# Edge counts in a graph network: own buffers, and a new spread of 565 small steps over three stages of the second layer's experts

## The chip, the cores and the metric

The kernel runs on one core of a Trainium2 chip. The metric is the device time of one execution in microseconds; lower is better. A core has five engines that run their own instruction streams in order: TensorE (PE, matrix products), VectorE (DVE), ScalarE (ACT), GpSimd (POOL) and SyncE (SP, which issues most transfers).

## The reference, cut to what matters

Four layers work on 3125 nodes with 256 features; each has a graph part over 50000 edges and a feed-forward part. The change touches the feed-forward part of the second layer and the counts that the graph part of the third layer needs.

```python
# second layer, feed-forward: the two best of 8 experts for each node
gate_logits = xf @ Wg + bg
top_w, top_i = jax.lax.top_k(gate_logits, 2)
top_w = softmax(top_w)
for e in range(8):
    h = gelu(xf @ W1[e] + b1[e])             # 256 -> 1024
    out += w_dense[:, e] * (h @ W2[e] + b2[e])   # 1024 -> 256

# third layer, graph: four convolutions over the same edges and self loops
deg = zeros(n).at[dst].add(1.0);  norm = rsqrt(deg)[src] * rsqrt(deg)[dst]
segment_sum((h @ W)[src] * norm[:, None], dst)
```

The third layer does not gather the edges again. It uses a table `c.adj` that holds, for each pair of source node and target node, how many edges join them (plus 1 on the diagonal for the self loop), and multiplies by it.

## The kernel before, in words

Nodes are kept in 25 tiles of 128 rows (`NT`, `P`), the running features in `c.x`.

*Feed-forward part of layer two* (`l1_ffn`). A row normalisation (`layernorm`) leaves `ys` and its transpose `c.yT`. `logits_of` computes the gate, `top8` picks the experts, and `route` works out, mostly on DVE, at which row of a buffer in DRAM each node's copy for its first and second expert belongs. `scatter_rows` then writes the rows there: 50 indirect transfers (`tbuf<-ys`), issued one after the other by POOL. `moe` walks over 32 blocks of 256 rows (`NS`, `ST`). Per block SP loads the expert's weights (`wa`, `wb`, 1 MB each) and the rows (`bx`); PE transposes the rows (`pbx`), DVE copies them to SBUF (`bT`); PE makes eight hidden chunks (`ph`, in `hidden`), ACT applies the gelu (`hT`); PE makes two output tiles of 8 products each (`po`), DVE adds the bias (`yo`), SP stores it (`obuf`). In the trace every such product of float32 data shows as two matmul records. After the loop 50 indirect fetches (`vr<-obuf`), issued by POOL, bring each node's two results back, and DVE adds them to `c.x`. After that the third layer begins with the row statistics of `c.x` (lines 158 and 159).

*Edge counts* (`adjacency`). 565 slots (`NSLOT`) of 128 edge records each have to be counted. A slot is a small chain: ACT makes `cdiff` and `cfrom` (one-hot rows of the sources), DVE makes `cto` (one-hot rows of the targets), PE multiplies them (`pcnt`, one record, 512 columns). The first 175 slots (`NFIX`) go to fixed places of `c.adj`: ACT writes the table. The other 390 go to places read from a list: DVE loads six registers at a time (`groups_of`) and adds the slot to the table with a read and a write (line 961). `work` is a Python generator: each `next(side, None)` emits one slot at that place of the program.

What sets the order: the text of the program gives the order of emission, and a scheduler of the framework then orders each engine's instructions by its own estimates, so that a slot can stand some way before or after the place where it was emitted. Before the change `moe` emits slots only in the block loop: one after each hidden chunk, one after every second product of an output tile and one after each tile, 18 per block, so that they run out in the last block. The slots' buffers (`cdiff` 3, `cfrom` and `cto` 6 each, `pcnt` 2 in PSUM) lie in the pools `wp` and `pp` of `moe`, in memory that `ys` held until the scatters had read it.

Of the kernel before, what the change touches and what calls it, by code (L numbers as in the profile page):

```python
# [17 lines left out]
PSUM = bass.MemoryType.PSUM  # L18
# [39 lines left out]
NFIX = NT * NDS  # L58
NMORE = (E - 1) // P
NSLOT = NFIX + NMORE  # L60
LOG2 = math.log(2.0)
BIG = 1.0e30
GROUP_BOUND = "a node tile's index is a sum of at most 24 comparisons"
# [695 lines left out]
def moe(c, I, pre, rows, exi, w0, w1, hid, beside=None):  # L759

    nc, tc = c.nc, c.tc
    w1n, b1n, w2n, b2n = pre
    mc = hid // P
    SR = ST // P
    with tc.tile_pool(name="moe1", bufs=1) as cp:
        with tc.tile_pool(name="moeps0", bufs=1, space=PSUM) as pp:
            b1 = load_cols(c, cp, pp, I[b1n], "b1c")
        with tc.tile_pool(name="moe", bufs=2) as wp, tc.tile_pool(name="moeps", bufs=2, space=PSUM) as pp:  # L770
            side = beside(wp, pp) if beside else iter(())
            for b in range(NS):
                (es,) = groups_of(c, exi, b, 1, SPE, NEXP - 1)
                (ev,) = groups_of(c, exi, b, 1, DVE, NEXP - 1)
                wa = wp.tile([P, KD, hid], F32, name="ew1")
                wb = wp.tile([P, mc, D], F32, name="ew2")
                b2 = wp.tile([P, D], F32, name="eb2")
                nc.sync.dma_start(
                    wa, I[w1n][bass.ds(es, 1)].rearrange("o (c p) n -> p (o c) n", p=P)
                )  # L780
                nc.sync.dma_start(
                    wb, I[w2n][bass.ds(es, 1)].rearrange("o (c p) n -> p (o c) n", p=P)
                )
                nc.sync.dma_start(b2, I[b2n][bass.ds(es, 1)].to_broadcast([P, D]))
                bc = wp.tile([P, mc], F32, name="eb1")
                nc.vector.tensor_copy(bc, at(b1.rearrange("p (e m) -> p e m", m=mc), ev))
                bT = wp.tile([P, KD, ST], F32, name="bT")
                for s in range(SR):
                    bx = wp.tile([P, D], F32, name="bx", bufs=4)
                    r0 = b * ST + s * P  # L790
                    nc.sync.dma_start(bx, c.tbuf[r0 : r0 + P, :])
                    pt = pp.tile([P, KD, P], F32, name="pbx", bufs=2)
                    for k in range(KD):
                        nc.tensor.transpose(pt[:, k, :], bx[:, k * P : (k + 1) * P], c.ident)
                    nc.vector.tensor_copy(bT[:, :, s * P : (s + 1) * P], pt)  # L795
                hT = wp.tile([P, mc, ST], F32, name="hT")
                for m in range(mc):
                    hidden(
                        c, pp, hT, wa, bT, ST, m,
                        lambda o, i, m=m, bc=bc: nc.scalar.activation(o, i, AF.Gelu, bias=bc[:, m : m + 1]),  # L800
                        bufs=2,
                    )
                    next(side, None)
                for s in range(SR):
                    po = pp.tile([P, D], F32, name="po", bufs=2)
                    for m in range(mc):
                        nc.tensor.matmul(po, hT[:, m, s * P : (s + 1) * P], wb[:, m, :], start=(m == 0), stop=(m == mc - 1))  # L807
                        if m % 2:
                            next(side, None)
                    next(side, None)  # L810
                    yo = wp.tile([P, D], F32, name="yo", bufs=4)
                    nc.vector.tensor_add(yo, po, b2)
                    r0 = b * ST + s * P
                    nc.sync.dma_start(c.obuf[r0 : r0 + P, :], yo)
            for _ in side:
                pass
        with tc.tile_pool(name="moer", bufs=8) as wp:
            for t in range(NT):
                for ri, w in zip(rows, (w0, w1)):
                    v = wp.tile([P, D], F32, name="vr")  # L820
                    gather(c, v, c.obuf, ri[:, t : t + 1])
                    xt = c.x[:, t, :]
                    nc.vector.scalar_tensor_tensor(xt, v, w[:, t : t + 1], xt, op0=OP.mult, op1=OP.add)
# [88 lines left out]
def adjacency(c, keep):  # L912

    nc, tc = c.nc, c.tc
    W = DS * P
    c.adj = keep.tile([P, NT * NT + DS - 1, P], U8, name="adj")
    nc.gpsimd.memset(c.adj[:, NT * NT :, :], 0.0)
    rec = keep.tile([P, NSLOT, 4], F32, name="crec_s")
    nc.sync.dma_start(rec, c.rec_c[: NSLOT * P, :].rearrange("(p k) w -> p k w", p=P))
    ui = keep.tile([1, NSLOT], I32, name="cui")  # L920
    nc.vector.tensor_copy(ui, rec[0:1, :, 2])
    io = keep.tile([P, W], BF16, name="ciota")
    nc.gpsimd.iota(io, pattern=[[1, W]], base=-W // 2, channel_multiplier=0, allow_small_or_imprecise_dtypes=True)
    is_ = keep.tile([P, P], BF16, name="ciotas")
    nc.gpsimd.iota(is_, pattern=[[1, P]], base=0, channel_multiplier=0, allow_small_or_imprecise_dtypes=True)

    def work(wp, pp):
        def counts(k, n):

            d = wp.tile([P, P], BF16, name="cdiff", bufs=3)  # L930
            nc.scalar.activation(d, is_, AF.Abs, bias=rec[:, k, 0:1])
            a = wp.tile([P, P], BF16, name="cfrom", bufs=6)
            nc.scalar.activation(a, d, AF.Relu, bias=1.0, scale=-1.0)
            b = wp.tile([P, W], BF16, name="cto", bufs=6)
            nc.vector.tensor_scalar(b[:, :n], io[:, :n], rec[:, k, 1:2], None, op0=OP.is_equal)
            ps = pp.tile([P, W], F32, name="pcnt", bufs=2)
            return ps, a, b

        for g in range(NT):
            for s in range(NDS):  # L940
                nd = min(DS, NT - s * DS)
                n = nd * P
                ps, a, b = counts(g * NDS + s, n)
                own = g // DS == s
                nc.tensor.matmul(ps[:, :n], a, b[:, :n], start=True, stop=not own)
                if own:
                    o = (g % DS) * P
                    nc.tensor.matmul(ps[:, o : o + P], c.identb, c.identb, start=False, stop=True)
                d0 = g * NT + s * DS
                nc.scalar.activation(  # L950
                    c.adj[:, d0 : d0 + nd, :].rearrange("p a d -> p (a d)"), ps[:, :n], AF.Identity
                )
                yield
        for k0 in range(NFIX, NSLOT, 6):
            regs = groups_of(c, ui, k0, 6, DVE, NT * NT - 1)
            for j in range(6):
                ps, a, b = counts(k0 + j, W)
                nc.tensor.matmul(ps, a, b, start=True, stop=True)  # L958
                o = c.adj[:, bass.ds(regs[j], DS), :].rearrange("p a d -> p (a d)")

                nc.vector.scalar_tensor_tensor(o, o, 100.0, ps, op0=OP.min, op1=OP.add)  # L961
                yield

    return work
# [452 lines left out]

def l1_ffn(c, I, keep):
    nc, tc = c.nc, c.tc
    beside = adjacency(c, keep)  # L1420
    with tc.tile_pool(name="f1", bufs=1) as cp:
        w0 = cp.tile([P, NT], F32, name="w0")
        w1 = cp.tile([P, NT], F32, name="w1")
        with tc.tile_pool(name="f1y", bufs=1) as yp:
            ys = yp.tile([P, NT, D], F32, name="ys")
            c.yT = yp.tile([P, KD, NP], F32, name="yT")
            layernorm(c, residual=False, ys=ys)
            wg = load_w(c, yp, I["L1_ffn_Wg"], "wg")
            bg = load_rows(c, yp, I["L1_ffn_bg"], "bg")
            lg = logits_of(c, yp, wg, bg, "lg1f")  # L1430
            mx, xf = top8(c, yp, lg)

            ex = yp.tile([P, NT], F32, name="ex2")
            nc.vector.tensor_sub(ex, mx[:, :, 1], mx[:, :, 0])
            nc.scalar.activation(ex, ex, AF.Exp)
            nc.vector.tensor_scalar_add(w0, ex, 1.0)
            nc.vector.reciprocal(w0, w0)
            nc.vector.tensor_mul(w1, ex, w0)
            rows, to, exi = route(c, cp, xf)
            scatter_rows(c, ys, to, "L1 tokens")  # L1440
        moe(c, I, ("L1_ffn_W1", "L1_ffn_b1", "L1_ffn_W2", "L1_ffn_b2"), rows, exi, w0, w1, 1024, beside)


def aggregate(c, wp, pp, acc, table, f):
# [606 lines left out]
```

## Time and profile before

| | us |
|---|---|
| median of 3 runs | 6873.1 (6866.4 to 6880.27) |
| profiled execution, its own time | 6859.87 |
| span of the profiled execution | 6858.1 |
| first scatter of layer two issued | at 3833.15 |
| last scatter issued | at 3895.15 |
| first hidden product of the experts | at 3912.99 |
| last `yo` of the experts begins | at 4535.1 |
| last of the 50 fetched results is added, begins | at 4603.45 |

The last five rows are times from the start of the span, read from the timeline. Between the first scatter and the last added result lie 770 us, a ninth of the span. Busy times and waits of an engine are read within that stretch; the whole page's shares average over four layers with different limits.

### The profile page before, as it was taken

To read this page: it belongs to the slowest core of one execution; us is meant where nothing else is said; L and a number is where in the kernel's file an instruction comes from. 1 tells how busy PE (TensorE), PEld (TensorE's weight loads), DVE (VectorE), ACT (ScalarE), POOL (GpSimd) and SP (SyncE) were. 2 spreads that over 40 slices of the span, in tenths; PEclk is the share of its full clock that TensorE was granted. 3 is DMA by queue.
4 is the path that set the end of the run, shared out by engine and by line. 5 is a ranking of instruction groups with operands and counts; after the bars stand their busy time and mean duration, and the time that the engine had idled before them with its cause. 6 is when DMAs were issued, how large, how long until landed. Compare 5 with 4: busy or idle time off the path is not lost. (4 is left out here: it accounts for less than half of the span.)

```text
span 6858.1 us, 79775 instructions
## 1 busy us (share of the span) xinstructions
PE 5098.2 (74%) x22936; PEld 3293.1 (48%) x22945; DVE 3956.1 (58%) x11222; ACT 2190.3 (32%) x6415; POOL 2873.3 (42%) x2832
## 2 busy tenths in 40 slices
PE   5778877885225688888885499947989996777594
PEld 3334333463114455555552377734755554444353
DVE  7555665463613578888886248867421114787503
ACT  3223333201001355555552297731212232000120
POOL 2566666677452177777762200020000002777101
PEclk8667787798568888888885699978988998788697
DMA  8323444371226322222221244430000001445232
GB/s 211 96 93 123 149 146 127 129 246 62 98 77 192 107 68 70 68 70 68 70 48 39 96 144 139 141 102 1 1 2 18 10 10 57 129 130 124 74 98 62
DMA packets 386625, 634.00 MB, mean 92 GB/s; under 512 B 72756, under 2 KB 273816, under 8 KB 378886
## 3 DMA queue, kind: packets, MB, share of 16 engines
q1 hardware_dynamic: 248386, 348.59, 16.4%
q0 software_dynamic: 118368, 259.84, 14.2%
q10 hardware_dynamic: 19428, 20.37, 0.9%
q8 instruction: 191, 3.13, 0.2%
q14 instruction: 252, 2.06, 0.1%
HBM read 478.42 MB, written 150.13 MB: 92 GB/s over the span
## 5 line engine op out<-in xcount | busy, mean ns | idle before, releaser
L217 POOL DMA_INDIRECT g<-tab,src x880 | 893.1, 1015 | 474.7 <-issue 315.7
L566 PE MATMUL p<-wf,sT 128*128 128x256 f32 x1564 | 599.6, 511 | 175.8 <-DVE sT L198 103.6
L566 PEld LDWEIGHTS p<-wf,sT 128*128 128x128 f32 x1564 | 335.8, 242 | 422.8 <-DVE sT L198 155.1
L217 POOL DMA_INDIRECT g<-tab,idx x391 | 402.1, 1028 | 303.7 <-ACT brec L391 110.1
L335 POOL DMA_INDIRECT rec_c<-crec,cpos x440 | 450.7, 1024 | 134.1 <-issue 124.4
L335 POOL DMA_INDIRECT rec_a<-g,posi x391 | 403.0, 1031 | 220.6 <-issue 66.2
L1728 POOL MEMSET acc<- 128x6425 f32 x1 | 5.5, 5453 | 1122.4 <-DVE x L664 1122.4
L335 POOL DMA_INDIRECT rec_b<-brec,bpos x391 | 415.0, 1061 | 119.2 <-issue 119.2
L651 PE MATMUL ph<-bT,ew 128*128 128x256 f32 (+1 forms) x1536 | 436.4, 420 | 18.0 <-DVE bT L795 12.8
L217 POOL DMA_INDIRECT vr<-obuf,rri x100 | 95.1, 951 | 834.2 <-issue 826.9
L1096 DVE TENSOR_REDUCE tm<-pb 128x2 f32<-128x512 f32 x550 | 359.7, 682 | 33.6 <-PE pb L1092 33.5
L1595 PE MATMUL pagg<-t,adj 128*128 128x384 bf16 (+1 forms) x2500 | 341.4, 289 | 31.7 <-DVE t L1589 28.5
L651 PEld LDWEIGHTS ph<-bT,ew 128*128 128x128 f32 x1536 | 286.3, 191 | 149.8 <-issue 56.3
L664 DVE SCALAR_TENSOR_TENSOR x<-po,pr,x 128x256 f32<-128x256 f32 x200 | 94.3, 484 | 454.7 <-PE po L662 454.7
L1782 PE MATMUL ps<-g,oh 128*128 128x257 f32 x880 | 324.0, 523 | 20.2 <-DVE mrun L1103 11.4
L568 DVE SCALAR_TENSOR_TENSOR g<-p,wgt,g 128x256 f32<-128x256 f32 x391 | 187.0, 481 | 257.2 <-PE p L567 239.2
L807 PE MATMUL po<-ew,hT 128*128 128x256 f32 x1280 | 321.9, 380 | 0.0
L1296 ACT ACTIVATE g<-g 128x64 f32<-128x64 f32 x1320 | 320.8, 335 | 0.9
L1306 PE MATMUL ps<-g,oh 128*128 128x277 f32 x880 | 303.2, 481 | 15.0 <-ACT g L1296 7.0
L1280 PE MATMUL z<-xr,ohT 128*128 x1320 | 251.5, 298 | 69.5 <-DVE lrest L1010 50.5
L509 PE MATMUL p<-rT,wf 64*128 64x512 f32 x392 | 280.6, 822 | 28.3 <-DVE ssp_r L197 26.9
L961 DVE SCALAR_TENSOR_TENSOR adj<-adj,pcnt 128x512 f32 x390 | 266.6, 684 | 50.7 <-PE pcnt L958 40.9
(641 smaller groups left out, 11597.6 us busy)
## 6 DMA issues: line engine op xcount, KB each, us to landing
ew<-in_L_ffn_W_dram SPq DMA_DIRECT2D x64, 1024.0 KB
rb<-rec_a SPq DMA_DIRECT2D x55, 1032.0 KB
tt<-to_rows SPq DMA_DIRECT2D x110, 256.0 KB
a<-in_edge_attr_dram SPq DMA_DIRECT2D x85, 256.0 KB
ew<-in_L_ffn_w_dram SPq DMA_DIRECT2D x64, 256.0 KB
bx<-tbuf SPq DMA_DIRECT2D x128, 128.0 KB
obuf<-yo SPq DMA_DIRECT2D x128, 128.0 KB
ew<-in_L_ffn_w_dram SPq DMA_DIRECT2D x16, 1024.0 KB
```

What stands on the lines that cost most here:

```text
L217: return c.nc.gpsimd.indirect_dma_start(out=out, out_offset=None, in_=table, in_offset=bass.IndirectOffsetOnAxis(ap=idx, axis=0))
L335: st = nc.gpsimd.indirect_dma_start(out=rec, out_offset=bass.IndirectOffsetOnAxis(ap=posi[:, j : j + 1], axis=0), in_=rc[:, j, :], in_offs ...
L509: nc.tensor.matmul(p1, wf1[64 * h : 64 * h + 64, k * P : (k + 1) * P], rT[64 * h : 64 * h + 64, :], start=True, stop=True)
L566: nc.tensor.matmul(p2, sT[:, k, :], wf2[:, k, :], start=(k == 0), stop=False)
L651: nc.tensor.matmul(ph[:, :n], w[:, k, m * P : (m + 1) * P], inT[:, k, :], start=(k == 0), stop=(k == kc - 1))
L807: nc.tensor.matmul(po, hT[:, m, s * P : (s + 1) * P], wb[:, m, :], start=(m == 0), stop=(m == mc - 1))
L961: nc.vector.scalar_tensor_tensor(o, o, 100.0, ps, op0=OP.min, op1=OP.add)
L1096: nc.vector.tensor_reduce(to, pb.rearrange("p i k e -> p i (k e)"), AX.X, OP.max)
L1296: nc.scalar.activation(v[:, h, :], v[:, h, :], AF.Copy, scale=k.gh[:, j, h, C : C + 1])
L1306: nc.tensor.matmul(ps, oh[:, 2 * q + i, :], k.g[:, 2 * q + i, :], start=(i == 0), stop=(i == 1))
L1595: nc.tensor.matmul(ps, adj[:, g * NT + d, :], tab[:, g], start=(g == 0), stop=(g == NT - 1))
L1782: nc.tensor.matmul(ps, oh, k.g[:, j, :SW], start=(i == 0), stop=(i == 1))
```

## The change

The slots get pools of their own (`cw` in SBUF, `cps` in PSUM), opened in `l1_ffn` around everything, and the generator is handed to `moe` instead of being started there. 80 slots are emitted directly after the scatters (`SLOTS_FIRST`), 12 per block in the expert loop (384 together: one after each hidden chunk, and one after every fourth product of an output tile), and four before each tile's fetched results are added (100). What is left, one slot, follows at the end.

```diff
+SLOTS_FIRST = 80
 def moe(c, I, pre, rows, exi, w0, w1, hid, beside=None):
...
-            side = beside(wp, pp) if beside else iter(())
+            side = beside or iter(())
...
                         nc.tensor.matmul(po, hT[:, m, s * P : (s + 1) * P], wb[:, m, :], start=(m == 0), stop=(m == mc - 1))
-                        if m % 2:
+                        if m % 4 == 3:
                             next(side, None)
-                    next(side, None)
                     yo = wp.tile([P, D], F32, name="yo", bufs=4)
                     nc.vector.tensor_add(yo, po, b2)
                     r0 = b * ST + s * P
                     nc.sync.dma_start(c.obuf[r0 : r0 + P, :], yo)
-            for _ in side:
-                pass
         with tc.tile_pool(name="moer", bufs=8) as wp:
             for t in range(NT):
+                for _ in range(4):
+                    next(side, None)
                 for ri, w in zip(rows, (w0, w1)):
                     v = wp.tile([P, D], F32, name="vr")
                     gather(c, v, c.obuf, ri[:, t : t + 1])
...
 def l1_ffn(c, I, keep):
     nc, tc = c.nc, c.tc
-    beside = adjacency(c, keep)
+    with tc.tile_pool(name="cw", bufs=1) as wp, tc.tile_pool(name="cps", bufs=1, space=PSUM) as pp:
+        l1_ffn_beside(c, I, adjacency(c, keep)(wp, pp))
+
+
+def l1_ffn_beside(c, I, side):
...
             scatter_rows(c, ys, to, "L1 tokens")
-        moe(c, I, ("L1_ffn_W1", "L1_ffn_b1", "L1_ffn_W2", "L1_ffn_b2"), rows, exi, w0, w1, 1024, beside)
+            for _ in range(SLOTS_FIRST):
+                next(side, None)
+        moe(c, I, ("L1_ffn_W1", "L1_ffn_b1", "L1_ffn_W2", "L1_ffn_b2"), rows, exi, w0, w1, 1024, side)
+        for _ in side:
+            pass
```

The first layer's experts use the same `moe` without slots.

More of the change, by code (lines that the diff above doesn't have):

```diff
@@ L1419, in l1_ffn @@
     nc, tc = c.nc, c.tc
-    beside = adjacency(c, keep)
+    with tc.tile_pool(name="cw", bufs=1) as wp, tc.tile_pool(name="cps", bufs=1, space=PSUM) as pp:
+        l1_ffn_beside(c, I, adjacency(c, keep)(wp, pp))
+def l1_ffn_beside(c, I, side):
+    nc, tc = c.nc, c.tc
     with tc.tile_pool(name="f1", bufs=1) as cp:
```

## Prediction

> **What bounds the kernel now.** The page's chain of waits starts at 5094.94, after the stages that change, so I read them from the table by stretches, then the waits inside the expert loop, then the timeline for the time from one start to the next (the pitch), which is shorter than a duration where instructions overlap.
>
> ```profile
> 3833.00:3897.00 64.00, 0.00 (x0) 0.00 (x0) 0.86 (x6) 0.00 (x0) 48.03 (x50) 0.50 0.29 102
> 3897.00:3920.00 23.00, 13.01 (x41) 7.24 (x43) 7.46 (x25) 18.40 (x55) 0.00 (x0) 0.60 0.67 232
> 3920.00:4102.00 182.00, 178.46 (x840) 134.06 (x846) 67.22 (x211) 177.16 (x552) 0.00 (x0) 1.00 0.45 146
> 4102.00:4527.00 425.00, 405.22 (x1846) 306.88 (x1845) 374.53 (x878) 327.29 (x956) 0.00 (x0) 1.00 0.41 133
> 4540.00:4604.00 64.00, 0.00 (x0) 0.00 (x0) 29.85 (x83) 0.00 (x0) 46.31 (x49) 0.50 0.49 144
> ```
>
> Columns: length, then busy us of PE, weight loads, DVE, ACT, POOL, then PE's granted clock. Beside the scatters (row 1) only POOL works; in the expert loop (rows 3, 4) PE is full at clock 1.00; beside the fetches (row 5) POOL sets the pace, DVE is half free, PE and ACT are idle at clock 0.50. So the slots sit where PE has no room, and two stretches of 64 us stand nearly empty.
>
> ```profile
> DVE adj L961 <- PE pcnt L958: 40.5, 67, 0.9
> PE pcnt L958 <- DVE adj L961: 19.7, 65, 1.4
> PEld ph L651 <- DVE bT L795: 15.3, 20, 1.2
> ```
>
> Waits within row 4. 390 listed slots in groups of six make 65 register loads, and PE waits for DVE 65 times.
>
> ```profile
> 4303.53 0.68 DVE L961 SCALAR_TENSOR_TENSOR adj<-adj,pcnt 128x512 f32 x1
> 4304.13 0.35 DVE L935 TENSOR_SCALAR cto<-ciota,crec_s 128x512 bf16<-128x512 bf16 x1
> 4304.39 0.68 DVE L961 SCALAR_TENSOR_TENSOR adj<-adj,pcnt 128x512 f32 x1
> ...
> 4307.66 0.38 PE L958 MATMUL pcnt<-cto,cfrom 128*128 128x512 bf16 x1
> 4308.74 0.38 PE L958 MATMUL pcnt<-cto,cfrom 128*128 128x512 bf16 x1
> ...
> 4318.31 0.35 DVE L935 TENSOR_SCALAR cto<-ciota,crec_s 128x512 bf16<-128x512 bf16 x1
> 4319.56 0.69 DVE L961 SCALAR_TENSOR_TENSOR adj<-adj,pcnt 128x512 f32 x1 [0.90 <-PE pcnt L958]
> ...
> 4591.29 0.88 DVE L823 SCALAR_TENSOR_TENSOR x<-vr,w,x 128x256 f32<-128x256 f32 x2 [1.99 <-DMA vr<-obuf,rri]
> ```
>
> PE: four product records and one slot in 1.08 us, so 0.216 per record. DVE: `adj` 0.60 and `cto` 0.265 to the next start, 0.86 a slot; a result's addition 0.40 (0.88 for two of 0.48). Behind a register load `adj` comes 0.98 us later than DVE is free.
>
> ```profile
> 3961.83 0.54 ACT L933 ACTIVATE cfrom<-cdiff 128x128 bf16<-128x128 bf16 x2
> 3962.23 0.62 ACT L950 ACTIVATE adj<-pcnt 128x512 uint8<-128x512 f32 x1
> 3962.71 0.72 ACT L931 ACTIVATE cdiff<-ciotas,crec_s 128x128 bf16<-128x128 bf16 x2
> 3963.30 0.62 ACT L950 ACTIVATE adj<-pcnt 128x512 uint8<-128x512 f32 x1
> ```
>
> ACT per fixed slot: 0.20 + 0.48 + 0.295 = 0.975 us, about 0.95 with one narrow slot in seven.
>
> ```profile
> 3895.15 0.96 POOL L749 DMA_INDIRECT tbuf<-ys,rti  x1 [0.30 <-issue]
> 3911.23 1.11 PE L794 MATMUL pbx<-ident,bx 128*128 128x128 f32 x4 [2.85 <-DMA bx<-tbuf]
> 3912.99 3.02 PE L651 MATMUL ph<-bT,ew 128*128 128x256 f32 x8
> ```
>
> The experts start 17 us after the last scatter ends (3896.1): rows and weights have to land first.
>
> **The change, step by step.** The built program shows each engine's order. PE: 13 slots before the routing's products, 55 before the expert biases' transpose (`pcols`), 80 before the third hidden chunk, 463 before the last output product, 102 behind it. No matmul and no transfer is added; POOL's order is as before, SP only issues some row loads (`bx`) earlier.
>
> *Routing and scatters: +9.* The slots no longer wait for the scatters, so they mix into the normalisation and the routing. The first two `cdiff` pairs and `cfrom` stand before the normalisation's root on ACT, 7 `cto` (1.9 us) before its reciprocal on DVE: +2.4; ACT's copies of the transposed rows get 4 `adj`, 2 `cfrom`, 2 `cdiff` more: +3 in all. Before the routing's product PE has 9 more slots at ACT's pace (9 x 0.95 = 8.5, against 8 us that DVE needs there): +4.3 in all. 25 `cto` stand before the first scatter's index is ready, 28 before the second's. With 6 buffers, `cto` number k waits for product k-6, so DVE's routing, and with it POOL's queue, runs at ACT's slot pace: the second scatter starts 8.5 later.
>
> Here a rule speaks against the change: the Trainium skill, "SBUF — State Buffer", section "Who interferes with whom", has `tensor_scalar` in a two-port mode hold the port that GpSimd needs, one side blocking fully. No row shows `cto` beside POOL. The nearest is the first layer's scatters (1786 to 1860): with DVE 71.91 of 74 us busy on other forms, POOL issued 54 transfers, one per 1.37 us against 1.265 here. With about 30 `cto` (10 us busy) in 62 us the row gives 0.015 per scatter, +0.7; the rule at its worst 30 x 0.35 = +10. Below nothing it can't be. I take the row: +9; ends +3 and +20.
>
> *Expert stage: -39.* First the opening. `pcols` comes at 3909 and the rows at 3920 (the transfers are the same, 9 later); only 62 slots may stand ahead of the rows in PE's order, and before the third hidden chunk PE has 18 more slots at 0.95 plus ACT's table load and two gelus (2 us): 3939, 34 us after the last scatter, where 17 sufficed. From there PE has 2040 product records and 381 slots at 0.216 (523) and 116 transposes at an estimated 0.13 (15): 538. The same sum before, from 3912.99: 2048 and 553 records (562), 124 transposes (16), 1 for the diagonal: 579, against 622 measured, so 43 were stalls, 1.4 per block. With 12 slots instead of 18, and 1.9 us between slots in the output tiles, the waits behind register loads (19.7) nearly go; the wait for `bT` (about 0.5 per block: one bias addition 0.34, one `adj` 0.60, one copy 0.42 less the PE work in between) stays, and in the first eight blocks ACT needs 1.19 per hidden chunk against PE's 1.08. I take 0.9 per block, 28. Sum 34 + 566 = 600 against 639.4 from the last scatter to the last `yo`: -39; ends -84 (no stall, and the opening as before) and -22 (stalls as before).
>
> *Fetches and statistics: +56.* DVE's order from the last `yo` to the last row statistic holds 102 `adj` (61), 97 `cto` (26), 50 additions (20), 25 statistics (0.40 each, 10, all behind the slots now; before, 14 of them stood between the fetches), the casts and a 3.45 us reduction that stand there too (5.5): 122.5 us of pure pitch. The 50 fetches need only 50 x 1.27 = 64 beside it: POOL is no longer the bound. Waits come on top. The order is `adj`, add, `adj`, add, `adj`, three `cto`, `adj`, `cto`: the product behind the first of the three `cto` takes 0.59 at clock 0.50 (the row at 3900.98), so its `adj` is ready 1.1 to 1.2 after that `cto` starts, and DVE is there after 0.8: 0.3 x 25 = 7.5. First fetched result: 1. For the 17 register loads the rule in "DMA: Bandwidth & Descriptors", section "Latency and other measured facts", gives a floor of 600 ns, 10 us by it as an estimate; the row above gives 0.98, up to 17, where nothing is queued ahead, and under 0.34 where three `cto` are (4304.99). DVE has work queued here: I take 0.15, 2.5. Sum 133.5 against 77.5 (4535.5 to 4613.0): +56; ends +45 (pitch alone) and +75.
>
> The sum: +9 - 39 + 56 = +26. The profile's own time is 6859.87 and would become 6886; the median of the runs stands 13.2 above that profile, so I add to the median: 6873.1 + 26 = 6899. Nothing later changes but by that shift.
>
> **The rivals.** *It cancels (0.18).* DVE's waits beside the fetches stay at nothing (+45), the loop loses half of its stalls more (-50), routing +6: +1, 6874. For it: each term is at an end that the rows allow. Against: all three must be.
>
> *Faster (0.10).* In the expert stage TensorE is the only limit: no stall in the loop, and ACT ahead at the opening. Its price is 84; with +9 and +56 that gives -19, 6854. It decides from the point where the stage shortens by more than 79. For it: PE's rows 3 and 4 are nearly full already, and the waits listed make up most of the 43. Against: 18 slots of ACT work stand in order before the third hidden chunk.
>
> *The buffers free nothing (0.04).* If the early slots still waited for the scatters, 55 slots would run after them at 0.95 before `pcols`: +52 instead of +9, 6942. Against: they need only the records, which had landed by 3778.9.
>
> **How the numbers follow.** The forecast, slower, has 0.68 and spans 6887 to 6924. The likeliest single time is 6899. The range 6868 to 6924 takes in the cancelling case and leaves out most of the faster case and the last rival. About 0.2% (14 us) is what a measurement of this kernel can tell from no change: slower 0.68 + 0.04 = 0.72, same 0.18, faster 0.10.
>
> **What would show it.** In the profile of the changed kernel: the first scatter near 3840; the first hidden products near 3921 but the full pace of PE only near 3939; the last `yo` near 4505; `PE pcnt <- DVE adj` well under 19.7; DVE busy throughout the fetches, with the last addition some 115 us after the last `yo` and POOL waiting for DVE. The forecast is wrong if DVE has gaps of a microsecond for each result beside the fetches, or if the expert stage shortens by more than 70.

## The result and the profile after

The changed kernel takes 6924.6 us (median of 6 runs, 6910.4 to 6929.9), the kernel before 6866.3 us in the same series: a ratio of 1.0083 with a 95% interval of 1.0068 to 1.0098. It is slower by 58 us. The profiled execution has a span of 6924.5 us for 6858.1.

To see where the time went I cut both timelines at the same five events. "Start" is the end of the last row statistic in the second layer's normalisation, "root" the start of the third layer's `rstd` on ACT; the others are starts of instructions.

| stretch (us) | before | after | difference | predicted |
|---|---|---|---|---|
| start to first scatter | 52.90 | 58.61 | +5.7 | +9, with the next row |
| first to last scatter | 62.00 | 62.54 | +0.5 | |
| last scatter to last `yo` | 639.94 | 628.99 | -11.0 | -39 |
| last `yo` to root | 79.36 | 143.33 | +64.0 | +56 |
| sum | 834.20 | 893.47 | +59.3 | +26 |

The other 7.1 us between the two spans lie outside: 3.5 before the start and 3.6 behind the root. The layers there are the same in both kernels, and two profiles of the unaltered kernel before differ there by 1.7 and 4.7 us too. So the stage explains the difference, and one row stands out: the expert loop gained little more than a quarter of what was forecast.

The table by stretches, now of the changed kernel, with the windows moved to where its stages lie (only the third is the window used before the change):

```profile
3842.00:3906.00 64.00, 17.35 (x37) 3.74 (x37) 13.09 (x43) 34.18 (x101) 48.58 (x50) 0.50 0.28 101
3945.00:4080.00 135.00, 133.70 (x632) 104.79 (x631) 42.84 (x132) 118.88 (x359) 0.00 (x0) 1.00 0.48 149
4102.00:4527.00 425.00, 388.30 (x1802) 308.66 (x1802) 284.21 (x655) 258.94 (x727) 0.00 (x0) 1.00 0.44 140
4540.00:4660.00 120.00, 52.05 (x95) 10.89 (x95) 105.83 (x237) 58.27 (x179) 45.27 (x48) 0.50 0.26 76
```

Columns as before: length, busy us of PE, weight loads, DVE, ACT and POOL, then PE's clock. In the second row PE is busy for 134 of 135 us. In the third, in the blocks with listed slots, PE is busy for 388 of 425 us (405 before): it stands idle for 37 us where it had been 20, although the thinner slots were to leave it fewer waits. In the last row DVE, half idle before, is busy for 106 of 120 us, and POOL's 48 fetches take those 120 us.

The waits in the third row's window (us in total, times, longest):

```profile
DVE adj L962 <- PE pcnt L959: 72.6, 91, 1.2
PEld ph L653 <- DVE bT L797: 49.0, 23, 2.7
PE pcnt L959 <- DVE adj L962: 37.2, 23, 2.0
```

Before, `ph <- bT` stood at 15.3 us in 20 waits and `pcnt <- adj` at 19.7 in 65. Now both come exactly 23 times, about once a block, and each is long: something happens once in every block. One block border shows it, first on DVE, then on PE (start, duration, what was done; in brackets the idle time before and what the trace says ended it):

```profile
4307.73 0.42 DVE L813 TENSOR_TENSOR yo<-po,eb 128x256 f32<-128x256 f32 x1 [0.78 <-PE po L809]
4309.42 0.69 DVE L962 SCALAR_TENSOR_TENSOR adj<-adj,pcnt 128x512 f32 x1 [1.27 <-PE pbx L796]
4310.02 0.42 DVE L797 COPY bT<-pbx 128x256 f32<-128x256 f32 x1
...
4308.18 0.38 PE L796 MATMUL pbx<-ident,bx 128*128 128x128 f32 x2
4310.16 0.38 PE L959 MATMUL pcnt<-cto,cfrom 128*128 128x512 bf16 x1 [1.60 <-DVE adj L962]
4310.49 0.48 PE L653 MATMUL ph<-bT,ew 128*128 128x256 f32 x1
```

DVE stands idle for 1.27 us between the last `yo` and the next `adj`, then makes `bT`, for which the next block's products wait. The trace names `pbx` as what ended the wait, but that transpose was done 0.9 us earlier. In the built program's order a load of six registers lies there, which the trace does not list. The trace agrees by count: numbered from the first listed slot, the `adj` behind this gap is the first of a group of six in every block.

In experiments one to eight every kernel, the one before included, took 7850 to 8190 us, because other layers ran slower on the chip at that time, so their totals carry no verdict and I read them by the stretches above, with the clock at 1.00 in the loop unless I say otherwise; in that series the opening came some 3.5 us later and the fetches took some 6 us more than in the first profiles (85.63 us against 79.36 for the same fetches, in experiment seven).

### The profile page after: what moved, and what is told of

The parts are those of the page before. It is cut to its first block, busy times and chain, and to the rows that moved or that the text cites. A ratio compares the mean times of both kernels' runs of the same rounds, so it can differ in the third digit from the quotient of the medians.

```text
span 6924.5 us, 79758 instructions
## 1 busy us (share of the span) xinstructions
PE 5155.1 (74%) x22945; PEld 3302.8 (48%) x22945; DVE 3962.7 (57%) x11222; ACT 2204.4 (32%) x6415; POOL 2882.1 (42%) x2832
## 3 DMA queue, kind: packets, MB, share of 16 engines
q1 hardware_dynamic: 248386, 348.59, 16.5%
## 5 line engine op out<-in xcount | busy, mean ns | idle before, releaser
L1794 PE MATMUL ps<-g,oh 128*128 128x257 f32 x880 | 318.9, 514 | 18.5 <-DVE mrun L1104 11.0
L809 PE MATMUL po<-ew,hT 128*128 128x256 f32 x1280 | 304.4, 380 | 0.0
```

The costliest lines, as they stand in the source:

```text
L1794: nc.tensor.matmul(ps, oh, k.g[:, j, :SW], start=(i == 0), stop=(i == 1))
```

## The experiments

The theory: the loop kept its stalls because a register load stands once in each block between the last `yo` and the first `bT`. Twelve slots in a block and six to a load mean that a load falls at the same two places in all 23 blocks, and the count of early slots sets which. The rival: DVE and PE wait for each other in the loop wherever the load stands. "Stretch" below is the sum from start to root.

**One and five: one early slot less.**

```diff
-SLOTS_FIRST = 80
+SLOTS_FIRST = 79
```

> One early slot less (79 for 80), all else as in the changed kernel. In VectorE's order this moves one of the two register loads of each block from between the last yo and the first bT of the next block to behind the fifth addition of the hidden chunks. Theory (the loop kept its stalls because a register load stands at each block's border, ahead of bT): a block takes 17.8 us for 18.83 in the 23 blocks with listed slots, the stage is 24 us shorter, 6900. Rival (DVE and PE wait for each other in the loop wherever the load stands): a block stays at 18.8 us, 6924.

Measured: a block takes 17.47 us for 18.83, the loop 597.13 us for 628.99, the stretch 858.16 for 893.47. The place I had named for the load was wrong (it went directly behind the first `bT`, not into the hidden chunks; the first `adj` of a group stands there in every listed block), but it left the border:

```profile
5345.51 0.68 DVE L962 SCALAR_TENSOR_TENSOR adj<-adj,pcnt 128x512 f32 x1
5346.10 0.42 DVE L797 COPY bT<-pbx 128x256 f32<-128x256 f32 x1
5347.79 0.69 DVE L962 SCALAR_TENSOR_TENSOR adj<-adj,pcnt 128x512 f32 x1 [1.26 <-PE ph L653]
...
5346.24 0.38 PE L959 MATMUL pcnt<-cto,cfrom 128*128 128x512 bf16 x1 [0.24 <-DVE adj L962]
5346.58 1.56 PE L653 MATMUL ph<-bT,ew 128*128 128x256 f32 x6
```

DVE's gap is as long as before, 1.26 us, but it lies behind `bT`, and PE no longer sees it. The waits of this kernel in 385 us of its listed blocks:

```profile
PEld ph L653 <- DVE bT L797: 16.5, 22, 0.8
PE pcnt L959 <- DVE adj L962: 5.3, 22, 0.2
```

49.0 us in 23 blocks became 16.5 in 22, and 37.2 became 5.3. The same kernel was run once more for its total:

> The kernel of the first experiment again, for its total time: there a block took 17.47 us for 18.83 and the stretch from the second layer's normalisation to the third's was 24 us longer than before the change (for 59 in the changed kernel). Theory: the total is 24 us over the time before, a third of a per cent. Rival (the stage gives back later what it gains): 50 us or more over it, as the changed kernel.

Its median was 8083 us beside 8072 for the kernel before, in runs that scatter by 200 us: inconclusive. Its stretch was 858.16 us again, to the hundredth.

**Six: is it the place or the count?** `SLOTS_FIRST = 74`, fewer early slots but the load back at the border.

> 74 early slots: six fewer than in the changed kernel, so the register loads of six fall at the same places as there, one of them between the last yo and the first bT. Theory (the place of the load decides): a block takes 18.8 us again. Rival (fewer early slots, not the place, made the blocks of the first experiment short): 17.5 us or less.

Measured: 18.83 us a block, loop 621.89, and DVE's gap is back ahead of `bT`:

```profile
5215.46 0.42 DVE L813 TENSOR_TENSOR yo<-po,eb 128x256 f32<-128x256 f32 x1 [0.78 <-PE po L809]
5217.14 0.69 DVE L962 SCALAR_TENSOR_TENSOR adj<-adj,pcnt 128x512 f32 x1 [1.26 <-PE pbx L796]
5217.75 0.42 DVE L797 COPY bT<-pbx 128x256 f32<-128x256 f32 x1
```

The place decides; the rival falls.

**Two: no slots beside the fetches**, 16 per block in the loop instead.

```diff
-SLOTS_FIRST = 80
+SLOTS_FIRST = 79
...
-                        if m % 4 == 3:
+                        if m % 2:
...
-                for _ in range(4):
-                    next(side, None)
```

> Against e1: no slot beside the fetches; 16 per block in the loop instead of 12, so that all 565 are done when it ends. Theory (beside the fetches a slot costs DVE's time in full): from the last yo to the last row statistic 77 us for 141, the loop's blocks grow by 4 records of 0.216 us and a little more stall, the last yo stays within 10 us of the changed kernel's; total 6867, as before the change. Rival (the loop has no room, a slot costs there what it costs beside the fetches, 0.64 us): the loop takes 60 us more and the total stays at 6900 to 6924.

Measured: the last `yo` to the root took 83.88 us (139.70 with 102 slots there, so 0.55 us a slot), the loop 633.31 (597.13): the 102 slots cost 56 us beside the fetches and 36 in the loop. Stretch 838.36, 4 us over the kernel before: the theory held. A side result: with 16 slots a block the load's place moves in a cycle of three blocks, and so does the time of a block, 18.39, 18.75 and 19.27 us in turn.

**Three: own buffers alone.** `SLOTS_FIRST = 0`, 18 slots per block, none beside the fetches.

> Own buffers alone: no early slots, 18 per block and none beside the fetches, as before the change. The program's order still puts 13 slots before the routing's products and 54 before the biases' transpose, since nothing holds them back, and leaves 3 instead of 18 in each of the next three blocks. Theory (routing and opening are late because the slots run ahead of them in the engines' orders, not because 80 of them are emitted there): first scatter 9 us later as in the changed kernel, opening some 6 us later, blocks 1 to 4 about 11 us shorter: 6866 to 6874. Rival (the count of early slots does it): first scatter as before the change, and 6860 or less.

Measured: first scatter at +58.67 (58.61 in the changed kernel, 52.90 before), loop 628.08, stretch 834.82. For the routing the theory held: it is late with no early emission at all. As the built order had it, the slots' own buffers let them run ahead of the routing; the 80 are not needed for that. For the opening it failed: block 0's last `yo` came 37.3 us after the last scatter (39.3 in experiment seven, which opens as the kernel before; 56.3 in experiment one). The late opening of the changed kernel does come from its early slots.

**Four: early slots that cannot run ahead of the routing.** As two, with 72 early slots; they read a copy of their records that hangs on the last result of the routing (`c.gate`), and `first`, the last early product, stands ahead of the biases' transpose and of the first rows' transposes in PE's order.

```diff
+        z = keep.tile([P, 1], F32, name="cgz")
+        nc.vector.tensor_scalar(z, c.gate, 0.0, None, op0=OP.mult)
+        rec2 = keep.tile([P, SLOTS_FIRST, 2], F32, name="crec_g")
+        nc.vector.tensor_scalar(rec2, rec[:, :SLOTS_FIRST, 0:2], z, None, op0=OP.add)
...
+            src = rec2 if k < SLOTS_FIRST else rec
...
-            nc.scalar.activation(d, is_, AF.Abs, bias=rec[:, k, 0:1])
+            nc.scalar.activation(d, is_, AF.Abs, bias=src[:, k, 0:1])
...
+        c.gate = last
...
+                with tc.issue_after(first):
+                    b1 = load_cols(c, cp, pp, I[b1n], "b1c")
```

> As e2, but 72 early slots that read a copy of their records made after the routing, so none can run ahead of it; and TensorE's orders put all 72 ahead of the biases' transpose. Theory: the first scatter is back at 3833 to 3836, the 72 slots fill the time of the scatters, and the experts start no later than before the change: against e2 some 15 us less, 6845 to 6855. Rival (the slots' cto beside the scatters hold POOL up, or ACT's pace sets the opening whatever the order): scatters at 1.35 us each or first products later than 3925, and 6865 or more.

Measured: half right. The first scatter is back at +52.88, and the 50 scatters took 62.26 us, so the 33 `cto` that ran beside them did not hold POOL up. But the first `ph` came 60.7 us after the last scatter (21 in its series), the loop took 667.67, the stretch 868.58. PE needed 118 us for 72 slots, 1.64 each, where ACT's work alone is 0.95: at clock 0.50 a slot's product takes 0.61 us, and for 27 us in all PE, DVE and ACT stood still together in gaps of 0.5 to 3.6 us. What those gaps wait for the trace does not show, and I did not settle it.

**Seven: fewer, larger register loads in the kernel before.**

```diff
-        for k0 in range(NFIX, NSLOT, 6):
-            regs = groups_of(c, ui, k0, 6, DVE, NT * NT - 1)
-            for j in range(6):
+        for k0 in range(NFIX, NSLOT, 26):
+            regs = groups_of(c, ui, k0, 26, DVE, NT * NT - 1)
+            for j in range(26):
```

> The kernel before the change with one edit: registers are loaded for 26 slots at a time instead of 6, so 15 loads for 65. Theory (the register loads make up most of the loop's stalls: a block takes 19.60 us of which PE's records and transposes fill about 18.2): a block takes 18.6 to 18.8 us, the loop is 18 to 24 us shorter, 6845 or a little more. Rival (a load takes time by the number of its registers, or DVE's 18 additions fill the block anyway): 19.5 us a block, within 5 us of the time before.

Measured: worse than both. Blocks without a load take mostly 18.7 to 18.9 us as the theory wanted, blocks with one up to 27; the loop took 722.17 us, 82 more than before (PE's clock was 0.92 in the listed blocks). Of the rival's two reasons the first is what the trace shows, a load that takes time by the number of its registers. DVE behind a load of 26:

```profile
5219.60 0.42 DVE L812 TENSOR_TENSOR yo<-po,eb 128x256 f32<-128x256 f32 x1
5225.94 0.69 DVE L961 SCALAR_TENSOR_TENSOR adj<-adj,pcnt 128x512 f32 x1 [5.92 <-issue]
```

**Ten: the other way, two registers to a load**, in the kernel before; the same three lines with 2 for 26.

> The kernel before with registers loaded for 2 slots at a time instead of 6: 195 loads for 65. In the seventh experiment DVE stood 5.13 us behind an addressed load of 26, against 0.85 to 0.98 behind one of 6, so about 0.21 us for each register. Theory (a load takes time by its registers, and a short one is hidden by the cto and additions already queued on DVE): a block takes 18.8 us for 19.60, the loop is about 20 us shorter. Rival (a load has a fixed cost that DVE sees each time): 9 loads a block instead of 3, 22 us a block, the loop 60 us longer.

Measured: a block takes 19.21 us for 19.60, the loop 627.45 for 639.72 (experiment nine), the stretch 822.15: the theory's direction, with 12 of its 20 us. The total is 6858.9 us beside 6865.7, ratio 0.9987, 0.9977 to 0.9997. The same place on DVE:

```profile
4313.86 0.42 DVE L812 TENSOR_TENSOR yo<-po,eb 128x256 f32<-128x256 f32 x1
4314.66 0.69 DVE L961 SCALAR_TENSOR_TENSOR adj<-adj,pcnt 128x512 f32 x1 [0.38 <-DVE yo L812]
```

At these places, from the start of `yo` to the start of the `adj` behind the load, it is 0.80 us with 2 registers, 1.69 with 6 (the block border above), 6.34 with 26. That is 0.22 to 0.23 us for each register, and by the same line 0.35 for none, which is `yo`'s own time to the next start (0.34). The loads do not get cheaper by being joined; they get longer than what DVE has queued to hide them.

**Eight: one slot per tile beside the fetches**, own buffers, no early slots, 17 per block.

```diff
+                    if s:
+                        next(side, None)
...
-                for _ in range(4):
+                for _ in range(1):
```

> Own buffers, no early slots, 17 per block, and one beside each of 21 tiles' fetches instead of four. Theory (beside the fetches DVE is half idle, so the first slot of each tile is free and only those over its idle time cost): from the last yo to the last row statistic 80 to 88 us, for 84 to 86 with none there and 141 with four. Rival (every slot there costs about 0.55 us, the slope between none and four): 97 us.

Measured: 89.92 us from the last `yo` to the root, for 85.67 in experiment three: 0.2 us a slot, between the two, nearer to the theory. From the last `yo` to the last addition it took 73.78 us (74.69 there), so the fetches themselves pay nothing. The loop took 617.73, the stretch 828.84.

**Nine: the kernel before again**, for its stages.

> The kernel before the change, unaltered, profiled in the same series as the other experiments, so that its stages can be set beside theirs. Every theory expects 640 us from the last scatter to the last yo within 4, and 79 to 86 us from there to the last row statistic (85.6 where the seventh experiment, whose fetches are the same, was read).

Measured: 52.92, 62.03, 639.72 and 79.56 us, 834.23 in all, 0.03 from the first profile. The later experiments are set beside these.

**Eleven: eight, held back from the routing** by the copy of four, for the first 66 slots, with no forced order.

> The eighth experiment with its first 66 slots reading a copy of their records that is made after the routing; no order is forced (28 slots stand before the biases' transpose). Theory: the first scatter returns to 53 us after the normalisation's statistics (58.6 there), the opening stays as it was, so the stretch from there to the third layer's statistics is 5 us shorter than the eighth experiment's 828.8, and about 20 us shorter than that of the kernel before in this series. Rival (with fewer slots done ahead, 39 for 66 at the end of the first block, what is saved on the routing comes back as fuller blocks): 829 or more.

Measured: first scatter at +52.94, loop 620.11, last `yo` to root 84.77, stretch 820.21. The total, 6860.6 us, is 0.9994 of that before (0.9986 to 1.0002): by itself not to be told from it. So the stretch's 14 us are not seen in full in the total; in the two profiles 6 of them are lost ahead of the start, and why is open. The last addition comes 68.64 us after the last `yo`, as in experiment nine (68.56); the 5 us more behind it go with the row statistics, of which 24 stand behind the last addition in the built order, for 9 in the kernel before.

**Twelve: eleven with two registers to a load.**

> The eleventh experiment with registers loaded two at a time, as in the tenth. Theory (the two gains add, since one is in the routing and beside the fetches, the other in DVE's waits in the loop): the loop 12 us shorter than the 620.1 there, 608, the stretch from the normalisation to the third layer's statistics 808 to 810 for 834.2 before the change, the total 20 to 26 us below the time before. Rival (with 17 slots a block the loads of six already lie where PE hardly waits, or the 21 slots beside the fetches pay for more loads): the stretch stays within 4 us of 820.

Measured: loop 607.09 us, stretch 804.47, total 6843.1 us beside 6864.2, ratio 0.9967 (0.9955 to 0.9980). The loop came as forecast, the stretch 4 us shorter than that, since the first scatter came 2 us earlier too (+50.69), and why is open. The gains add: 21 us faster than the kernel before and, by the two ratios, some 80 faster than the changed one.

## Why the prediction was right, and which term was mis-sized

The direction was right; the size was not: 58 us for 26. The time, 6924.6, lies at the very end of the range (6899 forecast, up to 6924), and that is in part luck: over the 6873.1 that the forecast started from, its end allowed 51 us, and the later runs of the kernel before brought that median down to 6866.3. Of the signs named, the first scatter (3842), the first hidden products (3922) and PE's full pace (3941) came within 3 us of the forecast; the last `yo` came at 4534 for 4505, and `pcnt <- adj` stood at 37.2 us where it should have been well under 19.7. By steps:

- *Routing and scatters, +9: +6.2.* The mechanism was right: experiment four takes the slots out of the routing and the delay goes. The rule against the change (`tensor_scalar` and GpSimd's port) was weighed by a row at +0.7 and at its worst at +10; the scatters took 0.54 us more with 35 `cto` beside them, so the row was the better guide. Whether `cto` runs in a two-port mode at all the trace does not show.
- *Opening, +17: +18.5.* Block 0's last `yo` came 53.5 us after the last scatter for 35.0. The mechanism was right: `pcols` came at 3909.76 (3909 forecast), the first rows' transposes at 3919.39 (3920), and 18 slots then stood before the third hidden chunk, at 3941.01 (3939). What the prediction did not say is that the time ahead of `pcols` goes to waste: the 55 slots that stand before it were done at 3880, and PE then waited in its order for the biases:

```profile
3877.96 1.03 PE L946 MATMUL pcnt<-cto,cfrom 128*128 128x512 bf16 x2 [0.89 <-ACT cfrom L934]
3909.76 0.34 PE L145 MATMUL pcols<-ident,b1c_r 64*128 64x64 f32 x1 [30.77 <-DMA b1c_r<-in_L_ffn_b_dram]
```

- *Loop, the step that failed: "the waits behind register loads (19.7) nearly go".* The expert stage shortened by 11 us, outside the term's own ends of 22 and 84 (with stalls as before, 34 + 538 + 43 = 615, the end should have read 24, not 22). Per block PE has 76 records of 0.216 us and four transposes (0.43 by this trace), 16.85 us. Forecast was 0.9 us of stall, 17.75 in all; measured 18.83, so 2.0 of stall, more than the 1.5 before the change (82 records, 18.14, measured 19.60). The missing 1.1 us in 23 blocks is 25 of the 28 us by which the stage missed. I had counted the register loads but not looked where they stand. Instead of nearly going, `pcnt <- adj` rose to 37.2 us and `ph <- bT` to 49.0. Experiments one and six show that the place alone makes 1.36 us a block, about the time of one load of six. With the load elsewhere the stall is 0.6 and the stretch 858.16, 24 us over the kernel before: what the prediction had said for the whole change, in a series whose other waits were some us longer.
- *Fetches, +56: +64.0.* DVE is the bound as forecast, from the first fetch to the last. The 17 register loads were put at 0.15 us each, 2.5 in all, because "DVE has work queued here". The trace has 17 gaps of over half a microsecond, one before every sixth `adj`, 13.9 us together. Two of them:

```profile
4563.97 0.69 DVE L962 SCALAR_TENSOR_TENSOR adj<-adj,pcnt 128x512 f32 x1 [0.72 <-DVE x L824]
4571.74 0.69 DVE L962 SCALAR_TENSOR_TENSOR adj<-adj,pcnt 128x512 f32 x1 [0.73 <-PE pcnt L959]
```

Those 11 us are more than the 8 by which this term missed; the other waits of DVE, put at 8.5, came to 1.9, and its pure pitch to 125.7 for 122.5. (Of the 25 statistics before the change, 16 and not 14 stood ahead of the last addition; the sum does not use that number.)

Both wrong terms are the same price. The prediction had set a floor of 600 ns for a load against an exposed 0.98 from one row, and had taken less than either. Experiments seven and ten show a price of 0.22 to 0.23 us per register and no such floor: two registers cost 0.45. The Trainium skill has a like price in "Runtime: NRT & Kernel Launch", section "Instruction fetch mechanics": about 200 ns per register even in bulk. It is given there for the loads that the runtime puts in; for this kernel's loads, which read a tile in SBUF, the measured 0.22 to 0.23 decides, and it is near. By the page's figure 17 loads of six are some 20 us (an estimate), of which the trace leaves 13.9 exposed.

Of the rivals, that it cancels fails on the fetches, which would have had to stop at +45, and on the expert stage, which would have had to shorten by 50 and did by 11. That TensorE is the only limit in the loop is refuted for this kernel, yet one slot less brings it close. The row of experiment one's listed blocks, PE's busy time in the second column:

```profile
5150.00:5535.00 385.00, 379.71 (x1765) 302.00 (x1764) 273.59 (x639) 248.73 (x705) 0.00 (x0) 1.00 0.48 155
```

That the own buffers free nothing is refuted by experiment three, where the slots run ahead of the routing.

## What to carry to other kernels

A load of registers stops the queue of its engine for a time by the number of registers, and the trace shows it only as idle time that it puts down to something long finished, or to nothing: find it in the program's order, keep it short, and put it behind what others wait for. When a loop's count and a group's size divide each other, the load falls at the same place in every pass, so one step more or less ahead of the loop can move the whole kernel. An engine that is half idle beside another's pace takes in a first small step cheaply and the next ones not: of a slot that takes DVE 0.86 us, the first per tile cost 0.2 us and the further three 0.6 each. What the first did cost came from work that the steps had pushed behind the end.

## What the runs showed of the hardware that I had not expected

Joining loads did not pay: 65 loads of six became 15 of 26, and the loop went from 640 to 722 us, while 195 loads of two made it 12 us shorter. And beside the scatters a slot that takes ACT 0.95 us took 1.64, with 27 us in which three engines stood still and the trace names no cause; this is open.
